# Layer two's first block of parts computed by the 40-product scheme on thirds of each batch's rows, and linear weights centred 14 slots later

## The chip, the cores and the metric

The kernel runs on one core of a Trainium2 chip. The metric is the device time of one execution in microseconds; lower is better. The median of three runs before the change is 2664.1 us (2662.74 to 2664.25). Engines: PE is TensorE (PEld its weight loads), DVE VectorE, ACT ScalarE, POOL GpSimd; SP issues most DMA transfers, in order.

## The reference, cut to what matters

```
h = relu(layernorm(x))                              # 128 batches x 64 rows x 768
for l in range(2):
    m_left, m_right = h @ W_left[l].T, h @ W_right[l].T
    u = where(j >= i, h_i . m_left_j, h_i . m_right_j) / sqrt(768)
    att = exp(u) * adj;  att = att / (sum_j att + 1e-10)
    ctx = att @ (h @ W_lin[l].T + b_lin[l])
    h = relu((ctx - mean) / (std + 1e-3) * a[l] + b[l])
out = x + h
```

All is float32.

## The kernel before

Tokens are kept transposed in parts of 256 columns (4 batches of 64 rows), `ht`, 768 features as three blocks of 2 x 128. `pass_one(l)` computes m_left and m_right and the attention of all 32 parts; `pass_two(l)` the linear product, the context and the normalisation, batch groups (units) `u` of 512 rows at a time, 16 of them. The order is layer one's pass one, pass two, then the same for layer two.

Pass one goes block by block over `SUPER`: block 0 has parts 0 and 1, each later one three parts. A block of three parts is a product of an 6 x 3 grid of weight blocks with a 3 x 3 grid of token blocks. The kernel computes it with the 40 products of `PRODUCTS`, each a weight sum ("form") times a token sum, and `READS`, which says to which of the 18 outputs `m` each product goes and with what factor. The results are four times too large, so the exponential is scaled by a quarter. Products accumulate in four chains, one PSUM bank each; a product may enter its bank when the reads of the product four places earlier are done. The first read of an output is a copy on ACT, the other ones are additions on DVE. Block 0 is plain: 36 products in 12 chains (`order`), and 12 copies on ACT. In layer two block 0 reads 18 raw weight blocks, loaded by `load_raw(1)` during the previous pass two, and the 40 forms, which were summed during layer one and stored in DRAM (`FORM`, tiles `g<-form`), are fetched while block 0 runs.

Token sums (`Tokens`, `T_OPS`, 38 per block) are made by POOL, with at most 11 alive; they, the forms, the linear weights and pass two's sums share 51 buffers `g` handed out first in, first out. The tokens of layer two come from DRAM and are scaled on ACT (`affine`); rows are transposed in blocks by DVE (`xb<-x`), stored, and reloaded as `ht`.

The order of all work beside the products is written by hand: `put(slot, f)` sets `f` at a slot, and each product runs two slots. `begins(k)` is the first slot of block k. After four products of a block come the scores of the block before (`sc<-m,ht`), then its softmax in eight steps. `idle` holds steps for slots in which nothing else is set. `final` sets the work of the last block of a pass one: the loads of the linear weights (`load_n`), their centring (`centre`: per group of three blocks three row sums on ACT, a mean on DVE, three subtractions on ACT), 17 sums of them in turn on POOL and DVE (`sums_n`), the bias, and the first token sums of pass two.

Of the kernel before, what the change touches and what calls it, by code (L numbers as in the profile page):

```python
# [17 lines left out]
def kernel(  # L18
# [158 lines left out]
    def begins(k):  # L177
        return 0 if k == 0 else 2 * PLAIN + 2 * len(PRODUCTS) * (k - 1)
# [398 lines left out]

    class Tokens:
        LIMIT = 11

        def __init__(self, l):
            self.l, self.ready, self.k = l, {0: 10 ** 9}, 1
# [6 lines left out]
        def value(self, k, v):  # L589
            if v < 9:  # L590
                return HT[1, self.l, SUPER[k][v % 3]][:, v // 3 * K2:(v // 3 + 1) * K2, :]
            return self.at[k, v]
# [7 lines left out]
        def emit(self, eng):  # L600
# [23 lines left out]

    def pass_one(l, start, final):
        with tc.tile_pool(name=f"one{l}", bufs=2, reuse_waits="tile") as sp, \
# [7 lines left out]
                      "m1": ([P, C, PB, 2, S], 1), "m2": ([P, C, PB, 2, S], 1),  # L634
                      "adj": ([P, 6, 2, S], 1), "wm": ([P, 6, 2, S], 1)}
            names = ("m0", "m1", "m2", "adj", "x", "xb", "wm") if l else ("x", "xb", "m0", "m1", "m2", "adj", "wm")
# [12 lines left out]
            M = [sp.tile([P, C, PB, 2, S], F32, name=f"m{i}", bufs=1) for i in range(3)]  # L649
# [4 lines left out]
            def product(bank, w, t, new, slot):  # L654
                p = bank.rearrange("p (g n) -> p g n", g=2)
                for g in range(2):
                    for c in range(K2):
                        nc.tensor.matmul(p[:, g], w[:, c, g * P:(g + 1) * P], t[:, c, :],  # L658
                                         start=(new and g == c == 0), stop=(c == K2 - 1), skip_group_check=True)
# [3 lines left out]
            def out_of(bank):  # L663
                return bank.rearrange("p (g b s) -> p g b s", g=2, s=S)

            def into(o):
                v, k, i = o // 6, o // 3 % 2, o % 3
                return M[v][:, i * K2:(i + 1) * K2, :, k, :]

            def scores(k):  # L670
                nq = 2 * len(SUPER[k])
                p = KEEP["scores"].rearrange("p a (q m) -> p (a q) m", m=P)
                for q in range(nq):
                    ht, m = HT[1, l, SUPER[k][q // 2]], M[q // 2]
                    for c in range(C):
                        for h in range(PAIR):
                            b = q % 2 * PAIR + h
                            mb = m[:, c, b].rearrange("p k j -> p (k j)")
# [5 lines left out]
            def chain(k):  # L684
# [23 lines left out]
                nc.scalar.activation(v, v, AF.Exp, scale=ISTEMPER if k == 0 else ISTEMPER / 4)  # L708
# [64 lines left out]
            weights, tokens = Weights(() if l else W_OPS, 2, True), Tokens(l)  # L773
            weights.at.update(W[l, "raw"])
            if l:
                weights.uses.update({b: 2 for b in range(18)})
                weights.uses.update({f: 1 for f in FORMS})
            fetch = list(range(len(PRODUCTS))) if l else []
            clock = {"pool": 0.0, "vector": 0.0}

            def turn_of(slot):
                now = slot * 0.86
                clock["vector"] = max(clock["vector"], now - 1.0) + sum(getattr(f, "vector", 0.0) for f in plan.get(slot, ()))
                run(slot)
                if fetch and slot >= start["weights"] and slot % 3 and free:
                    i = fetch.pop(0)
                    t = weights.at[FORMS[i]] = free.popleft()
                    nc.sync.dma_start(t, FORM[i])
# [12 lines left out]
            def prepare(b, slot, step=1):  # L801
# [5 lines left out]
                for t in range(2):  # L807
# [4 lines left out]
                    lag = 22 if b > 2 else 16  # L812
                    if before >= 0:
                        at = max(at, begins(where[before][0] + 1) + 2 * SCORED + 3)
# [6 lines left out]
            if l:  # L821
                follow[1] = [14, 14]
                put_all(4, affine(1, l, 1))
            for b, at in [(b, start[b]) for b in ((2,) if l else (1, 2))] + [
                    (b, begins(1) + SPACE[l][b > 4][b % 3] + 160 * (b // 3 - 1)) for b in range(3, NB)]:
                put(at, lambda b=b, at=at: prepare(b, at, 1 if b < 3 else 2))

            order = [(0, 0), (1, 0), (0, 1), (1, 1)] + [(w, t) for w in range(2, 6) for t in range(2)]
            slot = 0
            for n, (w, t) in enumerate(order):  # L830
                bank = KEEP["XYZ"[n % 3]] if l else bank_of(n % CHAINS)
                for j in range(3):
                    tok = HT[1, l, t][:, j * K2:(j + 1) * K2, :]
                    product(bank, weights.at[3 * w + j], tok, j == 0, slot)
# [11 lines left out]
            for k in range(1, len(SUPER)):  # L846
                assert slot == begins(k)
                put_all(slot + 2 * SCORED + 4, softmax(k - 1), 3)
                put(slot + 2 * SCORED + 42, lambda k=k: load_adj(k, nc.scalar))
# [4 lines left out]
                def reads(i):  # L854
                    bank = out_of(bank_of(CHAINS * (k - 1) + i % CHAINS))
                    for o, c in READS[i]:
                        if o not in seen:
                            seen.add(o)
                            nc.scalar.activation(into(o), bank, AF.Copy, scale=float(c))  # L859
                        elif abs(c) == 1:  # L860
                            added(nc.vector, into(o), "+" if c > 0 else "-", into(o), bank)
                        else:
                            nc.vector.scalar_tensor_tensor(into(o), bank, float(c), into(o),  # L863
                                                           op0=ALU.mult, op1=ALU.add)

                for i, (f, t) in enumerate(PRODUCTS):
                    w, tok = weights.need(f), tokens.need(k, t)
                    product(bank_of(CHAINS * (k - 1) + i % CHAINS), w, tok, i < CHAINS, slot)
# [4 lines left out]
                    if i == SCORED:  # L873
                        scores(k - 1)
                    if i >= SCORED:
# [84 lines left out]
    def pass_two(l, aside):  # L960
        last = l == L - 1
        with tc.tile_pool(name=f"two{l}", bufs=2, reuse_waits="tile") as sp, \
# [246 lines left out]
            for u in range(NB):  # L1209
# [96 lines left out]
```

## Time and profile before

| | us |
|---|---|
| median of three runs | 2664.1 |
| profiled execution, its own time | 2660.8 |
| its span, first to last instruction | 2659.0 |
| layer one, pass one, last block's first product | 778.5 |
| layer two, pass one, first product | 1340.9 |
| layer two, pass one, block 1 | 1403.2 |
| layer two, last block's first product | 2084.2 |

The profile is of one execution on the one core. Page rows of engines give busy time, share of the span and instructions. A row of a timeline has start, duration, engine, source line, operation, tiles (out<-in), shape and count, merged where equal instructions follow each other; in brackets stands the idle time before it and what ended it. A row of windows has, behind the bounds, the length, the busy us (and count) of PE, PEld, DVE, ACT and POOL, the granted clock of PE, the busy share of the DMA engines and GB/s. A row of groups ends with busy us, mean ns of one, and idle us before. Every product that is written once appears as two matmuls with two weight loads in the trace.

### The profile page before, as it was taken

Reading aid. Unit: us, or ns where it says so; the run is one execution under the profiler, and the core shown is the slowest. Engines: PE = TensorE matmul, PEld = TensorE weight load, DVE = VectorE, ACT = ScalarE, POOL = GpSimd, SP = SyncE. Lnnn points to the kernel's source line nnn. Section 1 sums busy time; section 2 is a strip of 40 time slices with the busy share of each in tenths; the row PEclk is TensorE's granted clock in tenths of the full one; section 3 lists DMA queues with packets and bytes.
Section 4 is the critical chain, followed back from the end, with each engine's and each line's share of the span. In section 5 each row is a group of like instructions: output and inputs, shape, how many; then the busy total and the mean of one; then the engine's idle time right before and its main releaser. Section 6 shows DMA issues by size and latency. Waiting matters only on the chain. (4 is left out here: it accounts for less than half of the span.)

```text
span 2659.0 us, 46920 instructions
## 1 busy us (share of the span) xinstructions
PE 2602.9 (98%) x18042; PEld 2219.6 (83%) x18042; DVE 1753.8 (66%) x2840; ACT 934.3 (35%) x1963; POOL 1726.7 (65%) x1328
## 2 busy tenths in 40 slices
PE   9899999999999999999999999999999989999998
PEld 8788888888887788888788888888888878888886
DVE  7877787777768445554415676677666675666667
ACT  5522223223213254454542222222222425455453
POOL 4766676666668557776225666667666567878786
PEclk9999999999999999999999999999999999999999
DMA  7443534343421344446795524353542215565655
GB/s 219 111 112 87 123 92 113 92 116 78 100 62 52 123 148 151 163 136 215 203 287 137 130 60 111 77 128 93 133 100 69 66 49 150 160 172 159 182 159 146
DMA packets 263358, 336.52 MB, mean 127 GB/s; under 512 B 56290, under 2 KB 195298, under 8 KB 263138
## 3 DMA queue, kind: packets, MB, share of 16 engines
q1 hardware_dynamic: 246338, 325.28, 44.5%
q10 hardware_dynamic: 16800, 8.26, 1.2%
q8 instruction: 144, 2.36, 0.4%
q14 instruction: 76, 0.62, 0.1%
HBM read 218.11 MB, written 115.34 MB: 125 GB/s over the span
## 5 line engine op out<-in xcount | busy, mean ns | idle before, releaser
L245 POOL TENSOR_TENSOR g<-ht 128x512 f32<-128x512 f32 x584 | 769.1, 1327 | 474.4 <-ACT ht L379 117.6
L245 POOL TENSOR_TENSOR g<-g,g 128x512 f32<-128x512 f32 x295 | 381.9, 1303 | 140.1 <-DVE g L245 39.3
L245 POOL TENSOR_TENSOR g<-ht,g 128x512 f32<-128x512 f32 x256 | 338.1, 1328 | 156.3 <-PE X L658 40.0
L658 PE MATMUL C<-g,g 128*128 128x256 f32 x1008 | 241.1, 382 | 10.0 <-POOL g L245 8.0
L954 PE MATMUL Z<-g,g 128*128 128x256 f32 x1024 | 244.1, 380 | 2.8 <-ACT hl L300 2.7
L658 PE MATMUL X<-g,g 128*128 128x256 f32 x1008 | 241.3, 383 | 4.9 <-DVE m L863 4.8
L658 PEld LDWEIGHTS C<-g,g 128*128 128x128 f32 x1008 | 191.1, 191 | 39.3 <-POOL g L245 11.1
L658 PE MATMUL Y<-g,g 128*128 128x256 f32 x912 | 217.3, 381 | 3.8 <-POOL g L245 3.8
L954 PEld LDWEIGHTS Z<-g,g 128*128 128x128 f32 x1024 | 191.6, 190 | 35.1 <-issue 4.1
L379 ACT ACTIVATE ht<-ht,b_col,a_col 128x256 f32<-128x256 f32 x384 | 196.5, 592 | 67.5 <-DMA ht<-h 59.5
L658 PEld LDWEIGHTS X<-g,g 128*128 128x128 f32 x1008 | 192.0, 191 | 33.5 <-DVE m L863 5.6
L658 PE MATMUL D<-g,g 128*128 128x256 f32 x880 | 209.2, 381 | 3.2 <-POOL g L245 3.2
L658 PE MATMUL Z<-g,g 128*128 128x256 f32 x864 | 204.7, 380 | 0.0
L658 PEld LDWEIGHTS Y<-g,g 128*128 128x128 f32 x912 | 174.3, 191 | 28.1 <-POOL g L245 4.2
L245 DVE TENSOR_TENSOR m<-m,D 128x512 f32<-128x512 f32 x180 | 118.2, 677 | 117.6 <-ACT m L859 99.2
L658 PEld LDWEIGHTS D<-g,g 128*128 128x128 f32 x880 | 167.6, 191 | 27.0 <-POOL g L245 4.0
L658 PEld LDWEIGHTS Z<-g,g 128*128 128x128 f32 x864 | 163.5, 190 | 23.1
L954 PE MATMUL X<-g,g 128*128 128x256 f32 x768 | 182.7, 379 | 0.0
L658 PE MATMUL V<-g,g 128*128 128x256 f32 x768 | 181.4, 379 | 0.0
L1154 POOL TENSOR_TENSOR z<-z,b 128x768 f32<-128x768 f32 x62 | 112.7, 1829 | 81.7 <-DVE z L1151 77.2
L954 PEld LDWEIGHTS X<-g,g 128*128 128x128 f32 x768 | 145.7, 190 | 20.6 <-issue 0.6
L658 PEld LDWEIGHTS V<-g,g 128*128 128x128 f32 x768 | 145.9, 190 | 19.8
(224 smaller groups left out, 4661.9 us busy)
## 6 DMA issues: line engine op xcount, KB each, us to landing
ht<-h SPq DMA_DIRECT2D x126, 768.0 KB, 6.2
h<-xb SPq DMA_DIRECT2D x124, 384.0 KB, 6.5
z<-z SPq DMA_DIRECT2D x128, 192.0 KB, 3.1
x<-z SPq DMA_DIRECT2D x128, 192.0 KB, 5.4
xr<-in_x_dram SPq DMA_DIRECT2D x120, 192.0 KB, 3.8
out_dram<-xr SPq DMA_DIRECT2D x120, 192.0 KB, 2.7
x<-in_x_dram SPq DMA_DIRECT2D x112, 192.0 KB, 5.5
g<-form SPq DMA_DIRECT2D x40, 256.0 KB, 5.1
```

What stands on the lines that cost most here:

```text
L245: (eng.tensor_add if sign == "+" else eng.tensor_sub)(o, a, b)
L379: nc.scalar.activation(ht, ht, AF.Relu, bias=cols[1][:, c:c + 1], scale=cols[0][:, c:c + 1])
L658: nc.tensor.matmul(p[:, g], w[:, c, g * P:(g + 1) * P], t[:, c, :], start=(new and g == c == 0), stop=(c == K2 - 1), skip_group_check=True)
L954: nc.tensor.matmul(p[:, n], b[t][:, c, r * P:(r + 1) * P], w[s][:, c, :], start=(i in FIRST and i not in PRELOAD and n == c == 0), stop=(c ...
L1154: nc.gpsimd.tensor_add(zs[k], zs[k], rows["b"])
```

## The change

Block 0 of layer two takes the 40 products too. Each batch's 64 rows are cut into three windows of 22 rows, beginning at 0, 21 and 42; the first row of the second and third is computed twice and dropped when read. A "part" of the scheme is now one window of all eight batches: two times 88 columns, 176 in all. A token sum is one tile of 176 columns; if one of its operands is a raw token, it is made in two calls, one for each real part. A product with a raw token is likewise issued once for each real part, with 88 columns. `m0` and `m1` become one tile `m`, so that a read covers both parts in one instruction.

The 18 raw blocks are no longer loaded. Of the 40 forms 12 are fetched in idle slots from unit 14 of layer one's pass two on, 8 in its last unit, the other 20 in block 0 itself; 11 token sums are made in the last unit. Layer two's later slots move by 8, as its block 0 has 80 slots instead of 72. In both layers the centring starts at slot 28 of the last block instead of 14, and the sums of the linear weights stand at 42 and every one and a half slots instead of 30 and every two.

```diff
-    def begins(k):
-        return 0 if k == 0 else 2 * PLAIN + 2 * len(PRODUCTS) * (k - 1)
+    def begins(k, l=0):
+        return 0 if k == 0 else 2 * (len(PRODUCTS) if l else PLAIN) + 2 * len(PRODUCTS) * (k - 1)
...
+    FIRST_OF = (1, 0)
+    WIDE, THIRDS = 22, ((0, 0), (21, 1), (42, 1))
+    CUT = PB * WIDE
...
+            j = v // 3
+            if k:
+                return [HT[1, self.l, SUPER[k][v % 3]][:, j * K2:(j + 1) * K2, :]]
+            r = THIRDS[v % 3][0]
+            return [HT[1, self.l, p][:, j * K2:(j + 1) * K2, :].rearrange("p c (b s) -> p c b s", s=S)[:, :, :, r:r + WIDE]
+                    for p in SUPER[0]]
...
-            added(eng, t, sign, self.value(self.k, a), self.value(self.k, b))
             self.at[self.k, v] = t
+            cut = a < 9 or b < 9
+            for o, x, y in zip(*(self.value(self.k, n, cut) for n in (v, a, b))):
+                added(eng, o, sign, x, y)
...
-            def into(o):
+            def into(o, thirds=False):
                 v, k, i = o // 6, o // 3 % 2, o % 3
+                if thirds:
+                    r, n = THIRDS[v]
+                    return both[:, i * K2:(i + 1) * K2, :, k, r + n:r + WIDE]
                 return M[v][:, i * K2:(i + 1) * K2, :, k, :]
...
-                now = slot * 0.86
+                now = slot * 0.86 if l == 0 or slot >= 80 else slot * 0.6 + 20.8
...
-                follow[1] = [14, 14]
-                put_all(4, affine(1, l, 1))
+                follow[1] = [24, 24]
+                put_all(10, affine(1, l, 1))
...
-            order = [(0, 0), (1, 0), (0, 1), (1, 1)] + [(w, t) for w in range(2, 6) for t in range(2)]
+            order = [] if l else [(0, 0), (1, 0), (0, 1), (1, 1)] + [(w, t) for w in range(2, 6) for t in range(2)]
...
-            for k in range(1, len(SUPER)):
+            for k in range(FIRST_OF[l], len(SUPER)):
...
+                    while l and f not in weights.at:
+                        fetch.popleft()()
                     w, tok = weights.need(f), tokens.need(k, t)
-                    product(bank_of(CHAINS * (k - 1) + i % CHAINS), w, tok, i < CHAINS, slot)
+                    product(bank_of(CHAINS * (k - 1) + i % CHAINS), w, tok, i < CHAINS, slot, TH if k else 2 * CUT)
...
-                    if i >= SCORED:
+                    if i >= SCORED or k == 0:
...
+                        put_all(2, [fetch.popleft() for _ in range(8)], 2)
+                        put_all(46, [lambda: TOKENS[1].step(0)] * Tokens.LIMIT, 1)
...
-            put_all(slot + 14, centre(l), 1)
-            put_all(slot + 30, sums_n(l), 2)
+            put_all(slot + 28, centre(l), 1)
+            for n, f in enumerate(sums_n(l)):
+                put(slot + 42 + 3 * n // 2, f)
...
+    def forms_first():
+        fetch.extend(load_forms())
+        later([fetch.popleft() for _ in range(12)], 1)
...
-    pass_two(0, {11: lambda: later(load_raw(1), 1)})
-    pass_one(1, {"weights": 3, "tokens": 50, 2: 10}, final_of(1))
+    pass_two(0, {NB - 2: forms_first})
+    pass_one(1, {"weights": 3, "tokens": 0, 2: 18}, final_of(1))
```

What this does to the order, at three places. PE at the start of layer two's block 0; before, `ht` of part 0 times raw weight blocks, three products to a chain:

```order
L658 MATMUL X_9235<-ht_8960,g17_131 128x256 x4
L658 MATMUL X_9235<-ht_8960,g45_159 128x256 x4
L658 MATMUL X_9235<-ht_8960,g46_160 128x256 x4
L658 MATMUL Y_9236<-ht_8960,g25_139 128x256 x4
L658 MATMUL Y_9236<-ht_8960,g26_140 128x256 x4
```

and now products 8 to 10, token sum times form, product 10 with a raw token of both parts (its eight rows read alike in pairs; four are shown):

```order
L702 MATMUL X_9236<-g40_154,g3_117 128x176 x4
L702 MATMUL Y_9237<-g14_128,g20_134 128x176 x4
L702 MATMUL Z_9238<-ht_8928,g12_126 128x88
L702 MATMUL Z_9238<-ht_8930,g12_126 128x88
L702 MATMUL Z_9238<-ht_8928,g12_126 128x88
L702 MATMUL Z_9238<-ht_8930,g12_126 128x88
```

The columns of a product fell from 256 to 176, or to twice 88, and a bank now comes back after four products, not after three chains. POOL in layer one's last block, around the first sums of the linear weights (`g5` is block 8, `g39` block 12, `g36` block 13); before:

```order
L245 TENSOR_TENSOR g32_146<-ht_5357,g41_155 128x512
L245 TENSOR_TENSOR g49_163<-g5_119,g39_153 128x512
L245 TENSOR_TENSOR g9_123<-ht_5308,g32_146 128x512
L245 TENSOR_TENSOR g5_119<-g5_119,g36_150 128x512
L245 TENSOR_TENSOR g29_143<-ht_5357,g15_129 128x512
```

and now:

```order
L245 TENSOR_TENSOR g32_146<-ht_5357,g41_155 128x512
L245 TENSOR_TENSOR g49_163<-ht_5308,g32_146 128x512
L245 TENSOR_TENSOR g9_123<-ht_5357,g15_129 128x512
L245 TENSOR_TENSOR g13_127<-ht_5308,ht_5357 128x512
L245 TENSOR_TENSOR g29_143<-g38_152,g7_121 128x512
L245 TENSOR_TENSOR g43_157<-g41_155,g7_121 128x512
L245 TENSOR_TENSOR g30_144<-g5_119,g39_153 128x512
L245 TENSOR_TENSOR g46_160<-ht_5364,ht_5357 128x512
L245 TENSOR_TENSOR g37_151<-ht_5357,g16_130 128x512
L245 TENSOR_TENSOR g5_119<-g5_119,g36_150 128x512
```

The sum that overwrites block 8 stands six token sums later. DVE at the same place, where its first weight sum (`g28<-g28,g5`) reads block 8; L228 and L229 are a group's mean. Before, behind the mean of the third group:

```order
L720 STREAM_TRANSPOSE wm_5792<-adj_5480 128x6x2x32
L228 TENSOR_REDUCE wmm_5607<-wm_5606 128x2
L229 TENSOR_SCALAR wmm_5607<-wmm_5607 128x2
L245 TENSOR_TENSOR g28_142<-g28_142,g5_119 128x512
L863 SCALAR_TENSOR_TENSOR m2_290<-C_279,m2_290 128x8x64 x2
```

and now ahead of it:

```order
L228 TENSOR_REDUCE wmm_5605<-wm_5604 128x2
L229 TENSOR_SCALAR wmm_5605<-wmm_5605 128x2
L245 TENSOR_TENSOR m0_288<-m0_288,Y_437 128x8x64
L914 SCALAR_TENSOR_TENSOR m1_289<-C_279,m1_289 128x8x64
L245 TENSOR_TENSOR m1_289<-m1_289,D_280 128x8x64
L245 TENSOR_TENSOR g28_142<-g28_142,g5_119 128x512
L971 TENSOR_REDUCE bs_5878<-bm_5877 128x1
L972 TENSOR_SCALAR bs_5878<-bs_5878 128x1
L914 SCALAR_TENSOR_TENSOR m2_290<-X_436,m2_290 128x8x64
L245 TENSOR_TENSOR m2_290<-m2_290,X_436 128x8x64
L228 TENSOR_REDUCE wmm_5607<-wm_5606 128x2
L229 TENSOR_SCALAR wmm_5607<-wmm_5607 128x2
```

The mean of the bias (L971, L972) has come in behind the sum, and the third group's mean after both.

More of the change, by code (lines that the diff above doesn't have):

```diff
@@ L623, with load_forms, load @@
     SPACE = (((0, 46, 97), (-12, 34, 97)), ((10, 46, 97), (10, 46, 97)))
+    TOKENS, fetch = [Tokens(l) for l in range(L)], deque()
+    def load_forms():
+        W[1, "raw"] = {}
+        def load(i):
+            t = W[1, "raw"][FORMS[i]] = free.popleft()
+            nc.sync.dma_start(t, FORM[i])
+        return [lambda i=i: load(i) for i in range(len(PRODUCTS))]
     def pass_one(l, start, final):
@@ L651, in pass_one, with product @@
+            M.append(sp.tile([P, C, PB, 2, S], F32, name="m2", bufs=1))
             other = [M[2].rearrange("p c b k s -> p (c b k s)")[:, g * 2 * H:(g + 1) * 2 * H].rearrange(
                 "p (k h) -> p k h", k=2) for g in range(2)]
-            def product(bank, w, t, new, slot):
-                p = bank.rearrange("p (g n) -> p g n", g=2)
+            def product(bank, w, ts, new, slot, n=TH):
+                p = bank[:, :2 * n].rearrange("p (g n) -> p g n", g=2)
                 for g in range(2):
@@ L677, in scores @@
                             b = q % 2 * PAIR + h
-                            mb = m[:, c, b].rearrange("p k j -> p (k j)")
+                            mb = both[:, c, q // 2 * PB + b] if l and k == 0 else m[:, c, b]
+                            mb = mb.rearrange("p k j -> p (k j)")
                             for e in (0, 32):
```

85 lines of the change are left out of this document (52 added, 33 removed).

## The prediction

> **What bounds the kernel now.** I read the page's first lines, then the windows of 10 us, then the timeline of the stretches that the change touches.
>
> ```profile
> span 2659.0 us, 46920 instructions
> PE 2602.9 (98%) x18042; PEld 2219.6 (83%) x18042; DVE 1753.8 (66%) x2840; ACT 934.3 (35%) x1963; POOL 1726.7 (65%) x1328
> ```
>
> TensorE sets the end: it is busy in 98% of the span, so time goes away in two ways only, by less work on PE or by fewer of the 56 us in which it stands. The change tries both, in different places. First the block that is recoded, layer two's first: start, duration and count of PE's merged rows.
>
> ```profile
> 1340.91 5.45 PE L658 MATMUL X<-ht,g 128*128 128x256 f32 x24
> 1397.99 5.34 PE L658 MATMUL Z<-ht,g 128*128 128x256 f32 x24
> 1403.17 1.89 PE L658 MATMUL C<-g,g 128*128 128x256 f32 x8
> ```
>
> It runs from 1340.91 (T0 below) to 1403.17: 62.3 us for 288 pairs of weight load and matmul (each written product shows as two), 0.216 us a pair, with no gap. Nobody is waited for there; only cheaper products help. Second, the last block of each layer, where the centring moves. The bracket is PE's idle time ahead of the row, and who ended it.
>
> ```profile
> 821.70 1.99 PE L658 MATMUL C<-g,g 128*128 128x256 f32 x8 [1.47 <-POOL g L245]
> 824.61 1.99 PE L658 MATMUL D<-g,g 128*128 128x256 f32 x8 [0.91 <-POOL g L245]
> 830.43 1.99 PE L658 MATMUL C<-g,g 128*128 128x256 f32 x8 [0.38 <-POOL g L245]
> 843.44 3.65 PE L658 MATMUL X<-g,g 128*128 128x256 f32 x8 [2.38 <-DVE m L863]
> 867.26 6.54 PE L680 MATMUL sc<-m,ht 128*32 128x95 f32 x265 [1.14 <-DVE m L245]
> ...
> 2121.34 1.99 PE L658 MATMUL D<-ht,g 128*128 128x256 f32 x8 [0.58 <-ACT m L859]
> 2130.24 3.62 PE L658 MATMUL C<-g,g 128*128 128x256 f32 x8 [3.45 <-POOL g L245]
> 2151.97 1.99 PE L658 MATMUL X<-g,g 128*128 128x256 f32 x8 [2.37 <-DVE m L863]
> 2174.30 5.81 PE L680 MATMUL sc<-m,ht 128*32 128x95 f32 x248 [1.14 <-DVE m L245]
> 840.00:850.00 10.00, 7.62 (x28) 6.06 (x28) 9.96 (x13) 0.83 (x2) 7.98 (x6) 0.83 0.00 0
> ```
>
> Two kinds of stand follow each other. One ends with POOL (2.8 us in layer one, 3.5 in layer two, and 0.6 with ACT), a second with DVE (2.4 each). After two of them the product takes 3.65 and 3.62 instead of the 1.9 of its neighbours, and the last row (the clock stands behind the counts) shows 0.83 granted: 1.7 us more each. Together 5.1 + 1.7 and 6.4 + 1.7, so 15 us, and 1.1 each at the scores. What holds POOL:
>
> ```profile
> 818.22 0.69 DVE L245 TENSOR_TENSOR g<-g,g 128x512 f32<-128x512 f32 x1
> 819.15 1.27 POOL L245 TENSOR_TENSOR g<-g,g 128x512 f32<-128x512 f32 x1 [7.85 <-DVE g L245]
> 2127.67 1.27 POOL L245 TENSOR_TENSOR g<-g,g 128x512 f32<-128x512 f32 x1 [10.67 <-DVE g L245]
> ```
>
> POOL stands 7.85 and 10.67 us before its second sum of linear weights, which overwrites block 8 and must let DVE's first sum read it. That sum stands in DVE's order behind the mean of the third group of blocks, which waits for ACT's centring. The token sums for the next products queue behind it on POOL, and PE runs out of them.
>
> **The change part by part.** *The recoded block, on PE.* 144 written products of 256 columns become 136 of 176 and 48 of 88 (six products read raw tokens, one call per part), so 272 and 96 pairs. The trace has no pair of these widths. Columns alone scale from 0.216 for 256: 0.148 for 176, 0.074 for 88. The load of 128x128 weights has to fit as well. Rows on it:
>
> ```profile
> 16.17 0.49 PE L446 MATMUL X<-ident,x 128*128 128x128 f32 x3
> 16.50 0.49 PE L446 MATMUL Y<-ident,x 128*128 128x128 f32 x3
> L658 PEld LDWEIGHTS X<-ht,g 128*128 128x128 f32 x280 | 53.1, 190 | 7.8 <-PE aux L996 0.6
> ```
>
> Three transposes with a full load each take 0.33, so a pair can go at 0.11 us; the loads' own rows say 0.190. I take 0.11 as the floor, since it is a rate that was reached, and 0.190 for the other end, as a load may be drawn out when there is time. Sum: 272 x 0.148 + 96 x 0.11 = 50.9 us, 11.4 less than 62.3; with 0.190 for all 368 pairs 69.9, 7.6 more.
>
> The Trainium skill ("TensorE: Matmul & The Clock Gate", section "Measured speedup vs the span model") says that a weight load overlaps running matmuls only when the row group differs, which would put load and columns one after the other here, as every tile takes all rows. This trace speaks against it: the pairs of 256 columns go at 0.216 with a load of 0.190 inside. By that rule and the transposes' 0.11 the block would take 272 x 0.258 + 96 x 0.184 = 88 us.
>
> *What feeds the block: POOL.* The 38 token sums are new work there, 26 of them in two halves of 176 elements, 12 whole with 352. Eleven are put into the last unit of layer one's second pass.
>
> ```profile
> L692 POOL TENSOR_TENSOR wm<-adj,tri 128x384 f32<-128x384 f32 x40 | 39.3, 1004 | 0.0
> L692 POOL TENSOR_TENSOR wm<-adj,tri 128x256 f32<-128x256 f32 x4 | 2.8, 732 | 0.0
> L245 POOL TENSOR_TENSOR g<-ht 128x512 f32<-128x512 f32 x584 | 769.1, 1327 | 474.4 <-ACT ht L379 117.6
> 1354.45 2.50 POOL L245 TENSOR_TENSOR g<-ht 128x512 f32<-128x512 f32 x2 [63.00 <-ACT ht L379]
> 1332.49 1.08 ACT L379 ACTIVATE ht<-ht,b_col,a_col 128x256 f32<-128x256 f32 x2
> ```
>
> From 384 and 256 elements: 2.13 ns an element and 0.19 us fixed, so 0.56 a half and 0.94 a whole, 26 x 1.12 + 12 x 0.94 = 40.5 us in all. POOL is idle for 63 us before 1354, so the eleven are free of charge; they can start when ACT has scaled the tokens, at 1333.6 (T0 - 7.3), and end at T0 + 4.5. PE asks for the 15th sum at T0 + 8.3 (seven products of 1.19) and gets it at 8.8; later ones come within a microsecond of their time. I charge 0.5 us. Bounds: 0, and what a half would cost if it took as long as a whole row of 512, 1.33; that is a rival below.
>
> *DVE and ACT.* The twelve copies become 84 reads of 336 to 352 elements, 18 on ACT and 66 on DVE.
>
> ```profile
> L245 DVE TENSOR_TENSOR m<-m,Y 128x512 f32<-128x512 f32 x184 | 120.5, 677 | 55.6 <-ACT m L859 34.1 <-PE Y L658 21.2
> L245 DVE TENSOR_TENSOR hl<-hl,Y 128x256 f32<-128x256 f32 x16 | 6.7, 417 | 10.6 <-PE Y L954 10.0 <-issue 0.3
> 1342.91 0.90 ACT L1159 ACTIVATE z<-aux,rs 128x768 f32<-128x768 f32 x1 [0.43 <-DVE rs L1147]
> 1346.88 0.60 ACT L379 ACTIVATE ht<-ht,b_col,a_col 128x256 f32<-128x256 f32 x1 [2.59 <-DMA ht<-h]
> 1347.39 0.56 ACT L840 COPY m<-X 128x512 f32<-128x512 f32 x1
> 1347.86 3.06 ACT L379 ACTIVATE ht<-ht,b_col,a_col 128x256 f32<-128x256 f32 x6
> 1350.92 1.28 ACT L767 ACT_TABLE_LOAD   x1
> 1357.15 1.84 DVE L465 STREAM_TRANSPOSE xb<-x 128x768 f32<-128x768 f32 x2 [1.36 <-DMA x<-z]
> ```
>
> On DVE a read costs 0.51 (between 0.417 for 256 and 0.677 for 512), 66 of them 34 us of the block's 51. The last four products hold 20 of them, 10.2 us, while PE still has three products (3.6) and the next block's first four (6.9) before the scores ask for them: even. The four row transposes wait for rows that landed at T0 + 16.2; they stand ahead of the reads of product 12, which product 16 needs at T0 + 20, so they are covered. ACT is tighter: the last row of pass two until T0 + 2.9, nine reads at 0.4, the table load, ten of the twelve scalings of parts 2 and 3 at 0.51, and only then the first read of product 7, at about T0 + 13.9, where product 11 wants its bank at 13.7. I charge 1 us.
>
> *Transfers.* Removed are 18 raw blocks, added nothing; 20 of the 40 sums move ahead of T0, 16 of them between the row loads and z stores of the last two units on SP's queue.
>
> ```profile
> 1320.00:1330.00 10.00, 8.07 (x41) 4.89 (x41) 3.92 (x9) 9.25 (x22) 0.00 (x0) 1.00 0.40 124
> 1330.00:1340.00 10.00, 9.84 (x53) 7.37 (x52) 4.28 (x12) 5.50 (x12) 0.00 (x0) 1.00 0.96 210
> 1350.00:1360.00 10.00, 10.00 (x48) 8.79 (x47) 3.67 (x4) 5.42 (x10) 2.50 (x2) 1.00 1.04 284
> 1352.90 5.55 SPq L788 DMA_DIRECT2D g<-form  x8
> ```
>
> The engines' share (next to last number) is 0.40 just before and 0.96 to 1.04 around T0. 16 x 256 KB are 4.2 MB, 15 us at 284 GB/s, into about 6 us of room in that row and whatever the units before leave: the reload of parts 2 and 3, which landed at T0 + 6.0, may land at 8.5. ACT stands before it at T0 + 8, and DVE's later reads follow: 1 us more, between 0 and 3. The other 20 sums start where they did, T0 + 12, at 0.7 us each, and are due from T0 + 25 on: covered.
>
> So this part gives 11.4 - 2.5 = 8.9 us.
>
> *The centring, in both layers.* Same instructions, 14 slots later; the sums from slot 42 every 1.5 slots instead of 30 every 2. In those slots (products 14 to 24) ACT has no first reads to delay; DVE's first sum now stands before the mean of the third group, and five token sums more stand before POOL's weight sums. The stands that end with POOL, with ACT, and the cold product behind the long one go: 2.8 + 3.5 + 0.6 + 1.7 = 8.6 us. The second kind I keep: DVE's eight sums are packed into 24 slots, and it was already full there (9.96 of 10 in the window quoted). I give 0.4 for all of it, 9.0 together. Bounds: the whole 15 + 2.3 = 17.3; on the other side eight slots of 0.86 less room per layer make DVE's last reads up to 6.9 us later, 13.8 - 8.6 = 5 us lost.
>
> Sum: 17.9. The profiled execution took 2660.8 against a median of 2664.1, so 2642.9 there and 2646.2 as a median; I say **2647**, rounded up.
>
> **The rivals.** *Only the block pays:* the weight sums' delay on POOL is handed to DVE's end of the block, and the last blocks stay as they are: 2664.1 - 8.9 = 2655. For it speaks DVE's full window. *The last blocks run through:* all 17.3 come back, 2664.1 - 26 = 2638. *The weight load sets the pair:* 0.190 each, the block 7.6 longer, the centring still 9 shorter: 2663, no change. The loads' rows speak for it, the transposes against it. *POOL becomes the bound, slower:* a half of a token sum costs 1.33 whatever its elements (short runs of 22). Then 64 instructions take 85 us, the last needed sum comes at T0 + 78, the block takes 82 us, 20 more: 2664 + 20 - 9 = 2675. It decides from a mean of 1.0 us per instruction on (64 us, where the block takes its old time) and turns the whole slower from 1.15; the rate of 2.13 ns an element speaks against it, which from 256 and 384 elements gives 1.28 for 512, where 1.33 is measured. The serial load of the skill's rule would end slower too; I give it 1 in 100, with the trace against it.
>
> **How the numbers follow.** Forecast 0.56 (its own range 2641 to 2653), only the block 0.17, both in full 0.08, weight load 0.07, POOL 0.07, other losses (a late transfer or DVE's end, the serial load) 0.05. A change of 0.2% (5.3 us) is what a measurement can tell: faster is below 2658.8 and takes the first three, 0.81; same 0.08; slower 0.11. For eight in ten the range goes from 2636 to 2663: it takes in the three gains and the weight load, and leaves POOL's case out.
>
> **What would show it.** In the new profile the first block's pairs at 0.148 (176) and 0.11 (88), its length 51 to 55 us, and POOL's halves at 0.56; PE's waits inside it few, ended by POOL near product 7 and by ACT near product 11. In the last blocks no wait of POOL for DVE over 3 us, no PE row behind POOL near product 16, and DVE's rows before the scores as late as before or a little later. Wrong it is if pairs of 88 take 0.19, if POOL's halves take over 1 us, if PE waits for a sum's transfer, or if the last blocks lose 15 us still.

## The result, and the profile after

| | before | after | ratio, 95% interval |
|---|---|---|---|
| first measurement, median of 7 runs each | 2664.1 | 2650.72 (2648.42 to 2657.35) | 0.9959 [0.9948, 0.9971] |
| again beside experiments (`e5_after_again`) | 2662.49 | 2654.67 | 0.9963 [0.995, 0.9977] |
| a third time (`e11_after_third`) | 2664.04 | 2652.56 | 0.9957 [0.9944, 0.9969] |

The kernel is faster by 0.4%, 10 to 12 us by the three ratios. (A ratio is not the quotient of the two medians beside it: by the medians the first measurement gives 13.4 us.) The profiled execution took 2648.42 us, the shortest of its seven. The page's first lines:

```profile
span 2646.6 us, 47202 instructions
PE 2591.6 (98%) x18122; PEld 2217.1 (84%) x18122; DVE 1780.6 (67%) x2888; ACT 935.4 (35%) x1969; POOL 1763.1 (67%) x1392
```

PE works 11.3 us less and stands 1.1 us less (55.0 of the span against 56.1). To see where, I cut the span at starts of PE's rows. In the timeline after, the cuts are the scores at the start of the last block and the first product behind the last scores, in each layer, and both ends of layer two's first block:

```profile
782.86 6.37 PE L733 MATMUL sc<-m,ht 128*32 128x95 f32 x288
868.79 1.56 PE L1006 MATMUL X<-g,g 128*128 128x256 f32 x6
1335.63 1.46 PE L702 MATMUL X<-g,g 128*128 128x176 f32 x8
1392.42 1.89 PE L702 MATMUL C<-g,g 128*128 128x256 f32 x8
2082.21 6.57 PE L733 MATMUL sc<-m,ht 128*32 128x95 f32 x288
2168.83 1.99 PE L1006 MATMUL X<-g,g 128*128 128x256 f32 x8
```

The same cuts in the other kernels' profiles (one execution each; the experiments are below):

| us between the cuts | before | after | e5 | e11 | e1 | e2 | e9 | e10 | e12 |
|---|---|---|---|---|---|---|---|---|---|
| layer one, last block | 89.56 | 85.93 | 87.62 | 85.68 | 89.81 | 86.44 | 85.95 | 86.66 | 88.82 |
| layer one, pass two | 465.85 | 466.84 | 467.56 | 468.66 | 468.32 | 466.45 | 466.52 | 467.01 | 466.87 |
| layer two, first block | 62.26 | 56.79 | 56.25 | 55.45 | 55.67 | 62.26 | 52.39 | 51.62 | 51.62 |
| layer two, last block | 90.13 | 86.62 | 88.22 | 87.38 | 91.96 | 86.97 | 87.24 | 86.70 | 91.85 |

The stretches that are not in the table have the same order in all kernels and differ by up to 4.5 us between these executions without a pattern. With the three profiles of the changed kernel averaged, against before: the first block gives 6.1, the last blocks 3.2 and 2.7, and pass two of layer one takes 1.8 back; 10.2 in all, as the ratios have it.

**The first block.** The products take what the columns ask; PE's rows of the new widths (the 88-column product is from two parts, so 16 pairs):

```profile
1336.93 1.36 PE L702 MATMUL Y<-g,g 128*128 128x176 f32 x8
1338.12 1.36 PE L702 MATMUL Z<-g,g 128*128 128x176 f32 x8
1347.67 1.91 PE L702 MATMUL Z<-ht,g 128*128 128x88 f32 x16
1351.17 2.30 PE L702 MATMUL V<-g,g 128*128 128x176 f32 x8 [1.59 <-POOL g L245]
1353.26 2.75 PE L702 MATMUL X<-ht,g 128*128 128x88 f32 x16
1355.85 1.39 PE L702 MATMUL Y<-g,g 128*128 128x176 f32 x8
1386.53 1.91 PE L702 MATMUL Y<-ht,g 128*128 128x88 f32 x16
1388.28 1.39 PE L702 MATMUL Z<-g,g 128*128 128x176 f32 x8
1391.15 1.43 PE L702 MATMUL V<-g,g 128*128 128x176 f32 x8 [1.47 <-DVE m L914]
1353.00:1356.00 3.00, 3.00 (x19) 3.00 (x19) 1.95 (x3) 0.47 (x1) 0.20 (x1) 0.67 1.10 225
```

From start to start 1.19 us for 8 pairs of 176 columns (0.149 each) and 1.75 for 16 of 88 (0.109). Product 11 (start 1351.17) was due at 1347.67 + 1.75 = 1349.42 and is 1.75 late; behind this stand products 11 and 12 take 2.09 and 2.59 from start to start instead of 1.19 and 1.75, with a granted clock of 0.67 in the last row: 1.7 more. Product 39 (1391.15) was due at 1388.28 + 1.19 = 1389.47: 1.7. These 5.2 us are what the block has over the 51.6 that it takes without stands (`e10_four_edits`, below).

The brackets mislead here. Product 11 waits for DVE and for POOL, and the bracket names POOL. The rows of ACT and DVE before it:

```profile
1345.33 0.60 ACT L379 ACTIVATE ht<-ht,b_col,a_col 128x256 f32<-128x256 f32 x1 [1.11 <-DMA ht<-h]
1346.16 4.03 ACT L379 ACTIVATE ht<-ht,b_col,a_col 128x256 f32<-128x256 f32 x8
1350.09 0.44 ACT L910 ACTIVATE m<-V 128x336 f32<-128x336 f32 x1
1350.57 0.50 DVE L245 TENSOR_TENSOR m<-m,V 128x336 f32<-128x336 f32 x1 [5.71 <-ACT m L910]
1346.60 0.93 POOL L245 TENSOR_TENSOR g<-g,g 128x352 f32<-128x352 f32 x1
```

The token sum of product 11 is the POOL row, done at 1347.53. Its bank, V, is free when product 7 is read: ACT's read stands behind ten scalings, these behind a reload that landed at 1345.3, and DVE's second read ends at 1351.07, 0.10 before PE starts. Product 39 has a form as its weights, and SP issues that form last (rows of SP's queue):

```profile
1374.60 10.19 SPq L361 DMA_DIRECT2D x<-z  x8
1384.90 0.36 SPq L651 DMA_DIRECT2D g<-form  x1
```

It is issued at 1384.90, behind eight row loads that hold the queue for 10 us, 4.6 us before product 39 is due. It lands 6.1 us after its issue (5.6 is the median of the 40 forms), at 1391.01, 0.14 before the product starts. DVE's last read of the bank was over at 1386.06, so here too the bracket names the wrong one.

**The last blocks.** The stands that ended with POOL are gone. (They stood at products 20, 21 and 24 as product 30 is counted here; the prediction says near 16.) POOL's waits of 7.85 and 10.67 us before its second sum are 3.59 and 3.37:

```profile
821.15 0.68 DVE L245 TENSOR_TENSOR g<-g,g 128x512 f32<-128x512 f32 x1
822.07 1.28 POOL L245 TENSOR_TENSOR g<-g,g 128x512 f32<-128x512 f32 x1 [3.59 <-ACT g L968]
```

The bracket names ACT, but POOL starts 0.24 us behind DVE's first sum, as it did before the change (818.22 + 0.69 and 819.15), so I take it for the same wait. A stand is left ahead of product 30, longer than before, and the one at the scores; layer one has 0.58 us more ahead of product 36. PE, then DVE just before:

```profile
837.23 1.99 PE L702 MATMUL X<-g,g 128*128 128x256 f32 x8 [2.90 <-DVE m L914]
860.36 3.59 PE L733 MATMUL sc<-m,ht 128*32 128x95 f32 x137 [1.14 <-DVE m L245]
2137.22 3.38 PE L702 MATMUL X<-g,g 128*128 128x256 f32 x8 [3.10 <-DVE m L914]
```

```profile
832.00 1.77 DVE L245 TENSOR_TENSOR g<-g,g 128x512 f32<-128x512 f32 x1
833.69 1.48 DVE L979 TENSOR_TENSOR g<-g 128x256 f32<-128x256 f32 x1
835.20 1.37 DVE L980 TENSOR_TENSOR g<-g,g 128x256 f32<-128x256 f32 x1
836.49 0.68 DVE L914 SCALAR_TENSOR_TENSOR m<-X,m 128x512 f32<-128x512 f32 x1
838.88 0.68 DVE L245 TENSOR_TENSOR g<-g,g 128x512 f32<-128x512 f32 x1
```

The read that frees bank X stands behind a weight sum and the two additions of the bias rows (L979, L980), as it did before the change.

### The profile page after: what moved, and what is told of

It is laid out like the page before. It is cut to its first block, busy times and chain, and to the rows that moved or that the text cites. A ratio compares the mean times of both kernels' runs of the same rounds, so it can differ in the third digit from the quotient of the medians.

```text
span 2646.6 us, 47202 instructions
## 1 busy us (share of the span) xinstructions
PE 2591.6 (98%) x18122; PEld 2217.1 (84%) x18122; DVE 1780.6 (67%) x2888; ACT 935.4 (35%) x1969; POOL 1763.1 (67%) x1392
## 5 line engine op out<-in xcount | busy, mean ns | idle before, releaser
L245 POOL TENSOR_TENSOR g<-ht 128x512 f32<-128x512 f32 (+1 forms) x620 | 785.9, 1279 | 420.8 <-PE Z L702 71.6
L245 POOL TENSOR_TENSOR g<-g,g 128x512 f32<-128x512 f32 (+1 forms) x310 | 397.9, 1291 | 136.7 <-PE C L702 22.0
L245 POOL TENSOR_TENSOR g<-ht,g 128x512 f32<-128x512 f32 (+1 forms) x272 | 346.1, 1282 | 164.8 <-PE Z L702 42.8
L702 PE MATMUL X<-g,g 128*128 128x256 f32 (+1 forms) x1080 | 252.9, 377 | 6.0 <-DVE m L914 6.0
L1006 PE MATMUL Z<-g,g 128*128 128x256 f32 x1024 | 244.1, 380 | 3.5 <-ACT hl L300 3.2
L702 PEld LDWEIGHTS X<-g,g 128*128 128x128 f32 x1080 | 203.0, 191 | 34.8 <-DVE m L914 6.8
L702 PE MATMUL Y<-g,g 128*128 128x256 f32 (+1 forms) x968 | 225.7, 376 | 3.8 <-POOL g L245 3.8
L702 PE MATMUL Z<-g,g 128*128 128x256 f32 (+1 forms) x936 | 217.0, 375 | 0.0
L702 PE MATMUL V<-g,g 128*128 128x256 f32 (+1 forms) x840 | 194.6, 375 | 3.1 <-POOL g L245 1.6
L1006 PE MATMUL X<-g,g 128*128 128x256 f32 x768 | 182.7, 379 | 0.0
```

The costliest lines, as they stand in the source:

```text
L245: (eng.tensor_add if sign == "+" else eng.tensor_sub)(o, a, b)
L702: nc.tensor.matmul(o, w[:, c, g * P:(g + 1) * P], t, start=(new and g == c == at == 0), stop=(c == K2 - 1), skip_group_check=True)
L1006: nc.tensor.matmul(p[:, n], b[t][:, c, r * P:(r + 1) * P], w[s][:, c, :], start=(i in FIRST and i not in PRELOAD and n == c == 0), stop=(c ...
```

## The experiments

There are twelve runs, two of them (e5 and e11) of the changed kernel again. Edits are shown against the changed kernel unless said otherwise.

**1 and 2. Each part alone.** `e1_centring_back` is the change with `centre` at slot 14 and the sums at 30 and every two; `e2_centring_only` is the kernel before with

```
-            put_all(slot + 14, centre(l), 1)
-            put_all(slot + 30, sums_n(l), 2)
+            put_all(slot + 28, centre(l), 1)
+            for n, f in enumerate(sums_n(l)):
+                put(slot + 42 + 3 * n // 2, f)
```

> The change with the centring and its sums put back to slots 14 and 30, so only layer two's first block is new. Theory A (the two parts add; the differences of 3.2 us in layer one before product 4 of the last block, and of 1 us in pass two, are scatter of single executions): block 56 to 58 us with stands of 1.5 us each at products 11 and 39, last blocks as before (82 to 83 us from product 4 to the row after the scores, POOL waiting 7 to 11 us for DVE), time 2664.1 - 5.5 to 7.5 = 2657 to 2659. Theory B (most of the gain belongs to the new block and the other layout of its tiles, the centring pays 0 to 2 us): 2651 to 2654.

> The kernel before with only the centring and its sums moved to slots 28 and 42. Theory A: last blocks 79 to 80 us from product 4 to the row after the scores, a stand of 2.5 to 3.5 us ended by DVE near product 30 left in each, first block of layer two 62.3 us, time 2664.1 - 6 to 7 = 2657 to 2658. Theory B: 2662 to 2664. By the term of the prediction (9.0) it would be 2655.

Measured: e1 0.9991 [0.9982, 0.9999], 2.4 us off 2664; e2 0.9975 [0.9965, 0.9986], 6.7 us. The sum, 9.1, lies within the error of the 10 to 12 of the change, so nothing speaks against the parts adding, and theory B falls: the centring alone gives most. The new block is worth less by itself than the 5.5 to 7.5 that theory A gave it: its stage shows 6.6 us (55.67), but in that execution pass two before it grows to 468.32 and layer two's last block to 91.96, 2.5 and 1.8 more than before.

**3. What product 11 waits for.** `e3_scalings_later`:

```
-                follow[1] = [24, 24]
-                put_all(10, affine(1, l, 1))
+                follow[1] = [34, 34]
+                put_all(20, affine(1, l, 1))
```

> The change with the twelve scalings of layer two's parts 2 and 3 put 10 slots later, so that ACT has two of them instead of ten ahead of its read of product 7. Theory: product 11 waits for its bank, whose first read stands on ACT behind scalings that wait for the late reload of part 2; then the stand of 1.59 us and the two slow products behind it (1.7 us) go, the block takes 53 to 54 us instead of 56.8, and the time is 3 to 3.5 us under the change's 2650.7. Rival (the trace names POOL as the releaser): the token sum of product 11 is late; then the stand and the slow products stay, gain 0.

Measured: 0.9969 [0.9956, 0.9981]. Product 11 starts on time behind product 10 (first two rows), POOL's order being unchanged, so it was ACT and not the token sum. But the 3 to 3.5 us did not come. The block takes 57.1: PE, now early, stands at product 16 and longer at product 39, where the bracket this time names the form and the product itself is slow.

```profile
1352.58 1.91 PE L702 MATMUL Z<-ht,g 128*128 128x88 f32 x16
1354.33 1.39 PE L702 MATMUL V<-g,g 128*128 128x176 f32 x8
1362.57 1.46 PE L702 MATMUL X<-g,g 128*128 128x176 f32 x8 [1.25 <-DVE m L914]
1395.15 2.69 PE L702 MATMUL V<-g,g 128*128 128x176 f32 x8 [2.27 <-DMA g<-form]
```

At product 16 DVE's read stands behind row transposes that wait for late rows:

```profile
1359.86 1.84 DVE L465 STREAM_TRANSPOSE xb<-x 128x768 f32<-128x768 f32 x2 [1.32 <-DMA x<-z]
```

The stand that was taken away alone was handed on to the next late transfer.

**4. What product 39 waits for.** `e4_rows_behind_form` moves the row loads, and with them nothing but their place on SP's queue:

```
-                    put(end + (8 if b == 2 else 0), lambda: load_rows(l, b + 1, sp))
+                    put(end + (8 + 8 * l if b == 2 else 0), lambda: load_rows(l, b + 1, sp))
```

> The change with the eight row loads of the next batches put 8 slots later, which moves them on SP's queue from ahead of the last form's fetch to behind it; nothing else moves on any engine. Theory: product 39 waits for the last of the forms, which SP issues at 1384.9 behind 10 us of row loads and which lands about 6 us later; with the fetch issued near 1375 the stand of 1.47 us ahead of product 39 goes, and the time is 1.5 us less than the change's. Rival (the trace names a DVE read as the releaser): DVE's reads are late for the bank; then the stand stays.

Measured: 0.9954 [0.9942, 0.9967]. The stand ahead of product 39 is gone; the product follows its neighbour by 1.23 us:

```profile
1391.87 1.39 PE L702 MATMUL Z<-g,g 128*128 128x176 f32 x8
1393.10 1.36 PE L702 MATMUL V<-g,g 128*128 128x176 f32 x8
```

The block takes 53.4 in that execution. Product 11 stood 0.62 us there, with 0.13 in which ACT waited for the reload; in e1, e9 and e11 ACT doesn't wait for it and product 11 stands 0.38, which is what ACT's queue costs alone. In time the gain can't be told from the change (ratios 0.9957 to 0.9963).

**5 to 8. The last blocks: may the bias rows' additions stand elsewhere?** `e5_after_again` is the changed kernel; `e6_bias_adds_later`:

```
-                put_all(slot + 40, work, 4)
+                put_all(slot + 40, work[:3], 4)
+                put_all(slot + 68, work[3:], 1)
```

`e7_bias_adds_on_pool` has `nc.gpsimd.tensor_add` for both; `e8_three_moves` joins e3, e4 and e6.

> The changed kernel itself, beside its variants on one chip. Theory (the two parts add, 6 to 8 us from the last blocks and the rest from the block, of which transfers take a part that differs between executions): 10 to 13 us under the kernel before of the same call; stand ahead of product 39 in the new block between 1 and 3 us, at product 11 between 0.4 and 2. If the 13.4 of the first measurement were scatter for the most part: 6 to 9.

> The change with the two additions of the bias rows (1.48 + 1.37 us on DVE, ahead of the read that product 30 of the last blocks waits for) moved to slot 68, still on DVE. Theory A (they make the stand at product 30, and there is room later): the stands of 3.1 us in each layer and the slow product (1.5) go, 5 to 7 us under the change. Theory B (DVE is busy without a break from product 26 to the scores, so it sets the block's end): the stand at product 30 shrinks under 0.5, but comes back at the row of the scores, 3 to 4 us instead of 1.1; gain 0 to 1.5.

> The change with the two additions of the bias rows on POOL at the same place. Theory A: 5 to 7 us under the change, as with the move to slot 68. Theory B: DVE has 2.85 us less to do in each last block and it sets the end, so 4 to 6 us under the change, while the move within DVE brings 0 to 1.5. If POOL's later token sums bound it instead: a stand ended by POOL near product 32 to 36, gain under 2.

> The change with the scalings 10 slots later, the row loads behind the last form, and the bias rows' additions at slot 68 on DVE. In the new block no stand at products 11 and 39, one of 0.6 to 1.3 us near product 18 (row transposes on DVE wait for their rows): block 52 to 53.5 us instead of 56.8. Theory A for the additions: 8 to 11 us under the change. Theory B: 3 to 5 us under it.

Measured side by side: e5 2654.67, e6 2653.73, e7 2653.36, e8 2650.39 us (ratios 0.9963, 0.9965, 0.9964, 0.9949, intervals about 0.0013 to each side). Theory A is wrong: neither place brings 5 us. PE of e6, then of e7:

```profile
845.64 1.97 PE L702 MATMUL C<-g,g 128*128 128x256 f32 x8 [1.04 <-POOL g L245]
853.35 1.97 PE L702 MATMUL C<-g,g 128*128 128x256 f32 x8 [0.56 <-DVE m L245]
866.88 3.36 PE L733 MATMUL sc<-m,ht 128*32 128x95 f32 x128 [2.39 <-DVE m L245]
```

```profile
842.90 3.40 PE L702 MATMUL C<-g,g 128*128 128x256 f32 x8 [2.52 <-POOL g L245]
```

Moved within DVE, layer one's 2.9 us come back as 0.3 left at product 30, 1.0 at product 32, where the token sum is next to be late, 0.3 at product 38 and 1.25 more at the scores (the 0.56 at product 36 stands in the changed kernel too). Moved to POOL they come back as 2.5 at product 32, this time behind POOL's token sums, with 0.3 left at product 30. So theory B is right of DVE, though the scores' stand grew to 2.4 and not to 3 to 4, and the bound on POOL that e7 named as its third case is right too: between 832 and 862 us of the changed kernel DVE is busy for 29.6 and POOL for 26.7 of 30 us. In e8 the first block took 54.8 us, not 52 to 53.5, with the stands at products 14 and 16 (1.56 and 1.09, ended by DVE) in place of 11 and 39. Its median is 4 us under e5, as theory B has it, but the intervals of the two ratios overlap.

**9 to 11. The forms ahead of the block.** Of the 20 forms fetched early, 8 are put into the last unit by slot. `e9_forms_earlier` lets all 20 go into idle slots from unit 12 on:

```
-        later([fetch.popleft() for _ in range(12)], 1)
+        later([fetch.popleft() for _ in range(20)], 1)
...
-                        put_all(2, [fetch.popleft() for _ in range(8)], 2)
...
-    pass_two(0, {NB - 2: forms_first})
+    pass_two(0, {12: forms_first})
```

`e10_four_edits` adds e3 and e4 to it, `e11_after_third` is the changed kernel.

> The change with the 20 forms that are fetched ahead of the new block all put into idle slots from unit 12 of layer one's pass two on, none into its last unit by slot. Theory (the forms fill the DMA engines in the last 35 us of that pass two, so the z stores and the reload of parts 2 and 3 come late): the share of the engines between 1320 and 1330 falls from 0.97 to 1.02 toward before's 0.40, ACT's waits for z (2.8 to 3.2 and 0.6 us) go back to before's 2.2 and none, pass two takes 466 to 466.8 us instead of 467.6 on average, the stand at product 11 is 0.4 to 0.7; 1 to 2.5 us under the change. Rival (the eleven token sums on POOL slow the end of pass two): the waits and 467.6 us stay, gain 0.

> The forms earlier as in the run beside it, the scalings 10 slots later and the row loads behind the last form. Theory: the block takes 52 to 53.5 us, with a stand of 0.6 to 1.5 us near product 18 only, pass two 466 to 466.8; 4 to 6 us under the change, about 15 under the kernel before. If the stands only move: the row transposes on DVE, near product 18, then hold PE for 2 to 3 us, gain 1 to 2.

> The changed kernel once more, for the comparison with the two runs beside it: 8 to 13 us under the kernel before, stands ahead of product 39 of 1.3 to 2.5 us and pass two 467 to 468.5 us.

Measured side by side, before at 2664.04: e9 2647.2 (0.9938 [0.9926, 0.9951]), e10 2647.6 (0.9937 [0.9924, 0.9951]), e11 2652.56. e9 is 5.4 us under the change, more than the 1 to 2.5 expected; its slowest run (2649.4) is below the fastest of e11 (2650.17). The window of 1320 to 1330 us after and in e9 (the DMA engines' share is the last number but one), and ACT's waits for the z stores in e11:

```profile
1320.00:1330.00 10.00, 9.07 (x44) 5.81 (x45) 3.03 (x7) 8.28 (x20) 2.12 (x5) 1.00 0.99 348
```

```profile
1320.00:1330.00 10.00, 7.66 (x39) 4.89 (x40) 2.27 (x6) 9.97 (x24) 0.00 (x0) 1.00 0.75 236
```

```profile
1317.56 0.81 ACT L1193 ACTIVATE z<-aux 128x768 f32<-128x768 f32 x1 [3.29 <-DMA z<-z]
1326.68 0.81 ACT L1193 ACTIVATE z<-aux 128x768 f32<-128x768 f32 x1 [0.71 <-DMA z<-z]
```

With the share at 0.75 the second of these waits is gone in e9 and e10. The first stays in e10 (3.26); in e9 ACT stands 2.77 us at its place, but for PE. Pass two takes 466.5 and 467.0 instead of 467.7 on average, so at least that part isn't the token sums'. The larger part came in the block, 52.4 in e9. There the last form is still issued behind the row loads, and still lands 6.1 us after its issue, but the whole queue is ahead: counted from the block's start it is issued at 44.8 us instead of 47.9 to 49.3 in the changed kernel's three profiles, and it lands 0.14 us before product 39 starts, just in time. The move takes load off the DMA engines and also off SP's queue, whose fetches of forms from 1310 to 1330 us take 9.8 us in e5 and 6.1 in e9; these runs don't separate the two. In e10 the block takes 51.6 with no stand over 0.3 us, against 50.9 for the bare products of the prediction. That the scalings' and the row loads' moves then bring nothing more in time fits this: they only cured what the crowded transfers made.

**12. Between the two places of the centring.** `e12_centring_at_22` is e10 with `centre` at slot 22 and the sums from 36.

> The version with four edits (forms earlier, scalings later, row loads behind the form), and the centring 6 slots earlier than the change has it: slot 22 and the sums from 36, so between before (14, 30) and the change (28, 42). Theory (DVE is full from the first weight sum to the scores and sets the end of the last blocks; a later start of the sums was paid with its room): the sums have 6 slots of 0.86 us more, the stand of 3.1 us near product 30 falls under 1.5 in each layer, nothing ended by POOL over 1 us comes back, and each last block takes 83 to 85 us by the stage table (86.6 and 86.7 at 28; 89.6 and 90.1 before), 3 to 7 us in all under the version with four edits. Rival (the stands that end with POOL return as soon as the sums come earlier): a stand of 1 to 4 us near products 16 to 20, the last blocks 86 to 89, gain 0 or a loss.

Measured: 2654.44, 0.9975 [0.9964, 0.9985], by the ratios some 10 us above e10. My theory fell, the rival holds: the stands that end with POOL are back (2.4 in layer one, 1.9 and 2.3 in layer two), POOL waits 5.03 and 6.73 us before its second sum, between the values of before and after, and the stand ahead of product 30 is hardly shorter.

```profile
826.42 2.57 PE L702 MATMUL X<-g,g 128*128 128x256 f32 x8 [2.41 <-POOL g L245]
845.23 1.99 PE L702 MATMUL X<-g,g 128*128 128x256 f32 x8 [2.37 <-DVE m L914]
```

So six slots of room for DVE are worth nothing there, and DVE did have idle stretches in that run (2.84 us before its sum at 837.12). With POOL's wait at 7.9 and 10.7, 5.0 and 6.7, 3.6 and 3.4 us for slots 14, 22 and 28, slot 28 is good because the sum that frees block 8 then stands where POOL doesn't hold up products, not because of DVE's load. Whether a place beyond 28 is better wasn't tried.

## Why the prediction was right, and which of its terms were off

The time alone would not have told the forecast (2647) from the rival that only the block pays (2655): by the three ratios the changed kernel stands at 2652.6 to 2654.2. It is e2 that does, with 6.7 us from the centring alone, and the stage table. The range of 2636 to 2663 held, but it was wide enough for three of the rivals as well; the block's length of 51 to 55 us, named as a sign, was missed (55.5 to 56.8). Term by term:

- **The products** (50.9 us for the block): right. 0.149 and 0.109 us a pair measured for 0.148 and 0.11, and 51.6 for the block once the stands were gone (e10). The rival of the 0.190 load is out: the 88-column pairs go at 0.109 while each load's row says 0.190, so successive loads overlap too. The sentence of the Trainium skill that a weight load overlaps running matmuls only where the row group differs ("TensorE: Matmul & The Clock Gate", section "The mechanism", not the one that the prediction names) does not hold here.
- **POOL's token sums:** right in price (0.538 us a half, 0.937 a whole, for 0.56 and 0.94), and the half microsecond charged at product 7 didn't come. The rows of groups after:

```profile
L245 POOL TENSOR_TENSOR g<-ht 128x176 f32<-128x176 f32 x36 | 18.2, 538 | 52.8 <-DMA g<-form 52.8
L245 POOL TENSOR_TENSOR g<-g,g 128x352 f32<-128x352 f32 x12 | 11.2, 937 | 0.5
```

- **ACT at product 11** (1.0): right in place. The stand is 0.38 us in the three profiles in which ACT doesn't wait for the reload (e1, e9, e11) and 0.6 to 0.7 in three in which it waits 0.1 to 0.2 (e4, e5, e7); the rest of the 1.75 is the reload.
- **Transfers** (1.0, bounds 0 to 3): this is the term that was mis-sized. The reload was feared at T0 + 8.5 and landed at T0 + 9.7 in the first profile (8.8 in e5, and before ACT asked for it in e11); there alone a slow clock followed the stand (1.7, not charged); the row loads came so late that the transposes held product 16 in eight profiles of the new block (0.4 to 1.3), where I had called them covered; and the last form, which I had called covered ("due from T0 + 25 on"), was issued behind ten microseconds of row loads, and product 39 stood 1 to 2.5 us in all seven profiles with that order of form and row loads and the forms in the last unit. What stands ahead on SP's queue I had counted for the reload only. And there was less room: the prediction goes by the share of 0.40 just before the block, but the last sixteen of the early fetches begin 27 to 29 us ahead of it (after, e5, e11), where the engines had none left. In the changed kernel's three profiles the stands come to 5.3 us on average instead of 2.5. The two windows ahead of the one with 0.40, before the change:

```profile
1300.00:1310.00 10.00, 10.00 (x56) 7.79 (x55) 3.57 (x8) 5.54 (x15) 0.00 (x0) 1.00 0.95 204
1310.00:1320.00 10.00, 9.95 (x55) 7.34 (x54) 4.78 (x13) 4.05 (x9) 0.00 (x0) 1.00 1.03 342
```

- **Pass two of layer one:** not in the sum at all. It takes 1.5 us more than in the two profiles without the new block, and kernels with the forms earlier get 0.9 of it back (466.8 on average of e9, e10 and e12).
- **The centring** (9.0): 5.9 us in the profiles against before, 6.7 by e2's ratio. The stands ended by POOL and ACT went as said, and the slow product behind the long one with them; but that product's 1.7 us belonged to one execution. In e1 the same stand is back, and the product behind it takes 1.99:

```profile
2127.26 1.99 PE L702 MATMUL C<-g,g 128*128 128x256 f32 x8 [3.45 <-POOL g L245]
```

  The second kind was kept in the sum at 2.4 a layer, with a little off, and grew to 2.9 and 3.1: DVE has the same work ahead of that read as before, and PE now comes to it without its earlier stands, so 0.5 to 0.7 us of each goes back there. And in layer two product 30 is slow now (3.38, 3.78 and 2.60 us in the changed kernel's three profiles, 1.9 at full clock); in layer one, where it was slow before, it takes 1.99, 3.78 and 2.00.

Together 6.1 + 5.9 - 1.8 instead of 8.9 + 9.0: the mechanisms were right, the range held, and the misses are on the side of the transfers. Of the signs named in the prediction, "if PE waits for a sum's transfer" came true, at product 39, and cost 1.0 to 2.1 us, not the gain as a whole. POOL's waits for DVE are 3.6 and 3.4 us, slightly over the 3 named.

## What to carry to other kernels

Work that is put into a stretch with idle slots for one engine may still be in a stretch without room on the DMA engines; look at their share there (0.95 and more in three of the four windows ahead of the block, before the change) before a fetch is moved, and at what stands ahead of each fetch on its queue, down to the last. When several waits in a row have one cause, late transfers here, curing one can hand its time to the next, and here only the cause paid: moving the twenty fetches earlier gave 5 us, each cure by itself nothing that the time could tell. Work that costs nearly the same stand on either of two engines, since both are nearly full there, gained nothing by a move from one to the other.

## What the runs showed of the hardware

- A stand of the same length is followed by products at full or at lower clock. Ahead of product 30 of layer two's last block PE stands 3.1 us in eight profiles; the product took 1.99 (e4, e10), 2.60 (e11), 3.38 (after), 3.41 (e3), 3.50 (e9) and 3.78 us (e2, e5), and the one behind it up to 3.1 instead of 1.9. The granted clock in the 4 us behind was 1.00 in e10 and 0.62 after:

```profile
2137.00:2141.00 4.00, 4.00 (x20) 3.17 (x19) 4.00 (x8) 0.00 (x0) 2.06 (x3) 1.00 0.00 0
```

```profile
2137.00:2141.00 4.00, 3.78 (x11) 3.14 (x12) 4.00 (x8) 0.08 (x1) 2.06 (x3) 0.62 0.00 0
```

  The Trainium skill ("TensorE: Matmul & The Clock Gate", section "What's actually happening") has the clock set by a window that runs free of the kernel. The scatter agrees with it; that the place of a stand in such a window decides was not tested here. In the sixteen stands of 2.9 to 3.1 us of these eight profiles (both layers) products 30 and 31 together lost 0.2 to 3.1 us, 1.5 on average. As an estimate from these, a stand of that length costs half as much again. The scatter may be part of why the changed kernel's seven runs spread over 9 us (before: 2.2); it wasn't shown.
- Sums on DVE with both operands in SBUF take 0.68 us alone and 1.77 next to POOL's sums (the rows at 832.00 and 838.88 above), and the 256-wide additions 1.48 and 1.37, longer than an uncontended 512; reads from PSUM of 512 stay at 0.68 (836.49, with POOL busy from 836.25 to 837.70). The Trainium skill ("SBUF — State Buffer", section "Who interferes with whom") says that a DVE instruction with two SBUF inputs contends with a POOL instruction that reads SBUF, and that one with at most one SBUF input, outside the two-port modes, does not. The trace agrees: 1.77 against 0.68 with two, 0.68 beside POOL with one.
